# Layer 0 of a four-layer network: impulse answers as small products, a woven expert front, norm sums at the writer, fills after attention

## The chip, the cores and the metric

One core of one Trainium2 chip runs the whole network in one launch. The metric is device time in microseconds (us), from the first to the last instruction of the execution. The engines are TensorE (PE: matrix products, PEld: its weight loads), VectorE (DVE), ScalarE (ACT), GpSimd (POOL) and SyncE (SP, which here only issues DMAs). Each engine works through its own instructions strictly in order; semaphores tie the engines together.

## The reference, cut to what matters

The input x has 32 sequences of 256 positions with 128 channels. Four layers each add an attention-like branch and an expert branch. The change touches layer 0 and the first lines of layer 1. In layer 0 the branches are:

- **Attention branch.** with xn the layer norm of x, `h` is a second layer norm of xn (with gamma and beta), and x becomes x + xn + y. y comes from h: a projection to three parts of 256 channels each, `u`, `v`, `g`. `u` goes through a depthwise convolution over 3 positions and a Silu, and then through a long convolution over time with one impulse answer per channel: `k_c(t) = sum over n of B[c,n] C[c,n] exp(-exp(A[c,n]) t)`, 64 states n, with `D[c]` added at t = 0. The result is gated (`y * sigmoid(g) + silu(v)`, the sigmoid made as (1 + tanh(g/2))/2) and projected by `out_w`. The reference writes the convolution as a scan over time: `s = s * eA + u * B; y = sum(s * C) + u * D`.
- **Expert branch.** A layer norm of x gives xn. A gate (`xn @ gate_w`, softmax over 16 experts) scores every token; each expert takes its 32 best tokens of each sequence, applies `Wd(gelu(Wg xn) * Wu xn)` with 256 hidden channels, scales by the score and adds it to those tokens. A shared expert of the same form runs on all tokens.

Layer 1's attention begins with a layer norm of x once more. The expert branches of layers 1 and 3 need tables of rows in DRAM ("slots") that start blank.

## The kernel before, in words

x stays in SBUF for the whole run, as 64 tiles of 128 tokens by 128 channels; a **block** is 4 tiles (2 sequences, 512 tokens), and there are 16 blocks. In `l0_attn` a `manual_schedule` (L497) keeps PE, ACT and DVE in the order in which the program is written; in `l0_ffn` a scheduler orders them before the change, which is why DVE's small constants (same_e, sel_b, rep) stand among the operations of the norm there. Waits come from the tiles: a pool with n buffers lets a name be written again when the reader of n writes ago is done, and a pool that is closed leaves its room to the next pool, whose first writers then wait for the last readers of the old one.

**Slots and fills** (`Slots.fill`, L274 to L282). The two slot tables are blanked by 56 DMAs of 260 KB, all issued by POOL. Each step is an `iota` into one of two blank tiles (L278) and a DMA from it (L282). The pool of the blank tiles is opened ahead of layer 0, and the call stands near the top of `l0_attn`.

**Norms** (`Norm`). `take` runs one `bn_stats` per tile (L214); `close(lo, hi)` turns the sums of the tiles lo to hi into mean and reciprocal root by some 20 small DVE operations (L220 to L248), 38 where the norm is a double one (`double=True`, which also gives r2). `ln_stats` is a take of all 64 tiles and one close. `normed` (L113) applies it to one tile, `transpose4` (L120) turns a block on PE.

**`l0_attn`.** Prelude: the loads; `a_t` through an Exp; `stats(0, 8)`; the products of the convolution's and the projection's weights (`wc`, L608); and small tables split in three bf16 parts. The impulse answers are made by `wave` (L571: an ACT Exp of 128x256 for each state n and half c of the channels) and `gather` (L578: a DVE multiply-add of it into `kk`), 64 of each for each half c, spread over loop 1 (c = 0) and loop 2 (c = 1). Each finished half goes to DRAM (`kpad`, L586), from where `fetch` (L675) reads it back in shifted rows. The loops over the 16 blocks are:

1. `prepare(blk)`: `normed`, x's own update on ACT (L632), transposes, and hT with gamma and beta (L638); then `project(0, blk - 1)`: 24 products with three shifts of hT (L652) and 4 with the bias rows (L655), and Silu into `us[0]` (L659). Between them stand a gather for each block, groups of waves, and the norm sums of the tiles 32 to 63 at block 2.
2. `project(1, blk)`, waves and gathers for c = 1, and `respond(0, blk)` (L685: 32 products with 32 columns of weights, tz fetched).
3. For c = 0 and 1: `gate` (v, g: L745, L746; Silu and Tanh, L749 and L751; z on DVE, L755 and L758), `give` one block later (L764 and L768 on PE, x's add on DVE, L773); for c = 0 also `respond(1, blk)`.

**`l0_ffn`.** A norm of all of x (`ln_stats`), then the gate for all 16 blocks (normed, transposes, xnT copied by ACT at L850, `lg` on PE at L852), one softmax; then four groups of 8 sequences, each `choose` (the 32 best by max, index and replace, L878 to L882, and a table `tab` of positions and scores, L887 to L901) followed by four `shared` blocks (g and u L911 and L912, gelu L913, product L914, o L918, x's add L923). Then for each of the 32 sequences the picking: `ib` (L955) spreads the chosen positions over the partitions, DVE turns it into 0/1 masks (`pick`, L962), and two products with xn gather the rows (`xg`, L965) into `xs` (ACT, L968). Then 16 experts in two halves each (L989 to L996), and the scattering (transposes L1008; `put` masks L1011, one of four on POOL; products L1019; x's add L1024). Layer 1 begins with a double `ln_stats` of x.

Of the kernel before, what the change touches and what calls it, by code (L numbers as in the profile page):

```python
# [19 lines left out]
P = 128  # L20
# [7 lines left out]
class Ctx:  # L28


    def __init__(self, tc, ins, es):
        self.tc, self.nc, self.ins = tc, tc.nc, ins
        nc = self.nc
        self.cp = es.enter_context(tc.tile_pool(name="persist", bufs=1))
        cp = self.cp
        self.x = cp.tile([P, NT, D], F32, name="x_sb")
        self.ident = cp.tile([P, P], F32, name="ident")
        make_identity(nc, self.ident)
        self.ones = cp.tile([1, P], F32, name="ones_row")
        nc.gpsimd.memset(self.ones, 1.0)  # L40

# [449 lines left out]
def l0_attn(K):  # L491
# [3 lines left out]
    with ExitStack() as es:  # L495
# [11 lines left out]
        a_t = K.load(sp, "a0_A", ins["a0_A"].rearrange("(c p) n -> p c n", p=P), [P, 2, NS])  # L507
        b_t = K.load(sp, "a0_B", ins["a0_B"].rearrange("(c p) n -> p c n", p=P), [P, 2, NS])
        c_t = K.load(sp, "a0_C", ins["a0_C"].rearrange("(c p) n -> p c n", p=P), [P, 2, NS])
        cols = K.load(sp, "a0_cols")  # L510
        gamma, beta = cols[:, 0:1], cols[:, 1:2]
        bias_v, bias_g, d_p = cols[:, 2:4], cols[:, 4:6], cols[:, 6:8]
# [8 lines left out]
        for n in range(3):  # L521
# [10 lines left out]
        tt = sp.tile([P, SEQ], F32, name="tt")  # L532
        nc.gpsimd.iota(
            tt, pattern=[[-1, SEQ]], base=SEQ - 1, channel_multiplier=0,
            allow_small_or_imprecise_dtypes=True,
        )
        kk = sp.tile([P, 2, KW], F32, name="kk")
        nc.gpsimd.memset(kk, 0.0)
# [10 lines left out]
        kpad = [dram.tile([P, KW], F32, name=f"kpad{c}") for c in range(2)]  # L549
# [6 lines left out]

        nc.vector.tensor_scalar_min(a_t, a_t, 69.0)
        nc.scalar.activation(a_t, a_t, AF.Exp)
        nc.vector.tensor_scalar_mul(a_t, a_t, -1.0)
        nc.vector.tensor_mul(b_t, b_t, c_t)  # L560
        nc.vector.tensor_scalar_mul(b_t, b_t, 0.5)
        for slots in (K.slots1, K.slots3):
            slots.fill(K.fill_pool)
        waves = {}

        def wave(c, m, pool):

            e = waves[c, m] = pool.tile([P, GC, SEQ], F32, name="tz")
            for i in range(GC):
                n = GC * m + i  # L570
                nc.scalar.activation(e[:, i, :], tt, AF.Exp, scale=a_t[:, c, n : n + 1])  # L571

        def gather(c, m):
            acc = kk[:, c, 0:SEQ]
            e = waves.pop((c, m))
            for i in range(GC):
                n = GC * m + i
                nc.vector.scalar_tensor_tensor(  # L578
                    acc, e[:, i, :], b_t[:, c, n : n + 1], acc, ALU.mult, ALU.add
                )  # L580
            if GC * m + GC == NS:
                k0 = kk[:, c, SEQ - 1 : SEQ]
                nc.vector.scalar_tensor_tensor(
                    k0, d_p[:, c : c + 1], 0.5, k0, ALU.mult, ALU.add
                )
                nc.sync.dma_start(kpad[c], kk[:, c, :])  # L586

        for m in range(6):
            wave(0, m, tp)
# [4 lines left out]
        def stats(lo, hi):  # L594
            for j in range(lo, hi, 8):
                norm.take(K.x, j, j + 8)
            norm.close(lo, hi)
            s = slice(lo, hi)
            nc.vector.tensor_scalar_add(r1[:, s], norm.r[:, s], 1.0)
            nc.vector.scalar_tensor_tensor(  # L600
                nb[:, s], norm.mean[:, s], -1.0, norm.r[:, s], ALU.mult, ALU.mult
            )

        stats(0, 8)


# [13 lines left out]
        es1 = ExitStack()  # L620
# [3 lines left out]
        ew = K.pool(es1, "a0ew", 4)  # L624
# [42 lines left out]
        def fetch(c, g):  # L667
            for q in range(2):
# [4 lines left out]
                    kpad[c].tensor, kpad[c].offset + c0 * KW, [[1, P], [KW, GC], [1, SEQ]]  # L673
# [26 lines left out]
        for m in range(2):  # L700
            gather(0, m)
        stats(8, 32)
        for blk in range(NBLK):
            if blk == 2:
                stats(32, NT)
            prepare(blk)
            if blk:
                project(0, blk - 1)
            if blk in (3, 7, 11):
                for m in range(blk + 3, min(blk + 7, NS // GC)):  # L710
                    wave(0, m, ew)
            if blk + 2 < NS // GC:
                gather(0, blk + 2)
# [3 lines left out]
        for blk in range(NBLK):  # L717
            project(1, blk)
            if blk in (0, 3, 6, 9):
                for m in range(blk * 4 // 3, blk * 4 // 3 + 4):  # L720
                    wave(1, m, ew)
            if blk < 12:
                for m in range(blk * 4 // 3, (blk + 1) * 4 // 3):
                    gather(1, m)
# [36 lines left out]
        def give(c, blk, z):  # L761
# [11 lines left out]
            nc.vector.tensor_add(xb, xb, o)  # L773

        last = None
# [14 lines left out]
def l0_ffn(K):  # L790
    nc, ins = K.nc, K.ins
    NE, CAP, F = 16, 32, 256
    ES = NE * CAP
    with ExitStack() as es:
        sp = K.pool(es, "f0", 1)
        xn = sp.tile([P, NT, D], F32, name="xn")


        idx = sp.tile([P, 4, CAP], F32, name="idx")
        tab = sp.tile([P, 4, 2, 8, 4], F32, name="tab")  # L800
# [4 lines left out]
        mean, r = K.ln_stats(sp, K.x, "f0")  # L805
# [7 lines left out]
        sel_b = sp.tile([P, 8, P], F32, name="sel_b")  # L813
# [20 lines left out]
        )  # L834

        with ExitStack() as ts:
            xp = K.pool(ts, "f0x", 1)
            wk = K.pool(ts, "f0w", 2)
            xnT = xp.tile([P, NBLK, 512], F32, name="xnT")
            sc = xp.tile([P, 2, NB, NE], F32, name="sc")  # L840
            with ExitStack() as ps:
                pt = K.pool(ps, "f0pt", 2, PSUM)
                pl = K.pool(ps, "f0pl", 1, PSUM)
                lg = pl.tile([P, 2, NB, NE], F32, name="lg")
                for blk in range(NBLK):
                    for j in range(4 * blk, 4 * blk + 4):
                        K.normed(xn[:, j, :], j, mean, r)
                    t = pt.tile([P, 512], F32, name="t")
                    K.transpose4(t, xn[:, 4 * blk : 4 * blk + 4, :])
                    nc.scalar.copy(xnT[:, blk, :], t)  # L850
                    for i in range(4):
                        nc.tensor.matmul(  # L852
                            lg[:, i % 2, 2 * blk + i // 2, :],
                            xnT[:, blk, i * P : (i + 1) * P], gate_w, start=True, stop=True,
                        )
                K.softmax(
                    xp, sc.rearrange("p h b e -> p (h b) e"), lg.rearrange("p h b e -> p (h b) e")
                )

            pt = K.pool(ts, "f0pt2", 1, PSUM)  # L860
            pg = K.pool(ts, "f0pg", 2, PSUM)
            po = K.pool(ts, "f0po", 2, PSUM)

            def choose(q):

                t = pt.tile([P, SEQ], F32, name="st")
                for h in range(2):
                    nc.tensor.transpose(
                        t[:, h * P : (h + 1) * P],
                        sc[:, h, 8 * q : 8 * q + 8, :].rearrange("p b e -> p (b e)"), K.ident,  # L870
                    )
                s = wk.tile([P, SEQ], F32, name="s")
                nc.vector.tensor_copy(s, t)
# [11 lines left out]
                nc.gpsimd.tensor_copy(idx[:, q, :], vi[:, 0, :])  # L885
                vt = pt.tile([64, P], F32, name="vt")
                nc.tensor.transpose(vt, vi.rearrange("p k s -> p (k s)"), K.ident)  # L887
                vs = wk.tile([64, P], F32, name="vs")
                nc.vector.tensor_copy(vs, vt)
                o = pt.tile([P, 2, P], F32, name="st")  # L890
                for k in range(2):
                    nc.tensor.matmul(
                        o[:, k, :], rep[:, k].rearrange("p a s -> p (a s)"), vs,
# [4 lines left out]
                    own, o.rearrange("p k (n a) -> p (k n) a", a=4),  # L898
# [6 lines left out]
            def shared(blk):  # L905
                h = wk.tile([P, 2, 512], F32, name="h")
                for c in range(2):
# [3 lines left out]
                    nc.tensor.matmul(g, wsg[:, cs], xnT[:, blk, :], start=True, stop=True)  # L911
                    nc.tensor.matmul(u, wsu[:, cs], xnT[:, blk, :], start=True, stop=True)  # L912
                    nc.scalar.activation(h[:, c, :], g, AF.Gelu)  # L913
                    nc.vector.tensor_mul(h[:, c, :], h[:, c, :], u)  # L914
                o = po.tile([P, 4, D], F32, name="o")
# [9 lines left out]
            for q in range(4):  # L925
                choose(q)
                for blk in range(4 * q, 4 * q + 4):
                    shared(blk)


        xs = K.pool(es, "f0s", 1).tile([P, 4, NB, 4, CAP], F32, name="xs")
        ew = K.pool(es, "f0e", 3)

        def expert(e):
            return (
                K.load(ew, "f0_wg", ins["f0_wg"][e]),
                K.load(ew, "f0_wu", ins["f0_wu"][e]),
                K.load(ew, "f0_wd", ins["f0_wd"][e].rearrange("(c p) d -> p c d", p=P), [P, 2, D]),
            )

        experts = [expert(0), expert(1)]
        with ExitStack() as ps:
            gw = K.pool(ps, "f0g", 2)
            pi = K.pool(ps, "f0pi", 2, PSUM)
            px = K.pool(ps, "f0px", 2, PSUM)
            for q in range(4):
                bd = gw.tile([P, NE, CAP], F32, name="bd")
                nc.gpsimd.tensor_mul(
# [1050 lines left out]
```

## Time and profile before

| | before |
|---|---|
| median of 3 runs | 3496.14 us (3491.07 to 3504.56) |
| the profiled execution | 3581.18 us |
| its span | 3579.2 us |
| its mean granted TensorE clock | 0.867 |
| PE, DVE, ACT, POOL busy in it | 2793.4, 1958.5, 1333.5, 821.4 us |
| layer 0 in it | 0 to 876 us (attention to 373, experts from there) |
| stages of attention: prelude; loop 1; loop 2; loop 3 c = 0; c = 1 | 0 to 52; to 156; to 245; to 326; to 372 |
| stages of experts: norm; gate; softmax, choice and shared; picks; experts; scatter | 372 to 392; to 437; to 532; to 622; to 796; to 876 |
| norm of layer 1 | 876 to 896 |

The profiled execution is one of many and took 85 us longer than the median; the durations are read from it. A line such as L768 is a line of the kernel; a group is written out<-in by the program's names, with the shape in partitions x elements. "idle before <-" names what ended the idle time of an engine ahead of an instruction. Idle time of an engine that others don't wait for costs nothing.

### The profile page before, as it was taken

The page shows a single profiled execution, that of the slowest core. Times are in us where ns is not written, and L with a number is a line of the kernel's source. Part 1 is how long each engine was busy: PE and PEld are TensorE (multiplying, and loading weights), DVE is VectorE, ACT ScalarE, POOL GpSimd, SP SyncE. Part 2 cuts the span into 40 slices and gives each one's busy share as a digit, 9 for nine tenths or more (in the row PEclk, how much of TensorE's full clock was granted, in tenths as well). Part 3 has the DMA queues.
Part 4 walks back from the last instruction along what each step waited for, and adds up shares of the span by engine and source line. Part 5 has one row for each costly group of instructions (what it writes and reads, how often), then busy time and mean ns, then how long its engine had stood idle before and what let it go on. Part 6 is the DMA issues. An engine that isn't in the chain of part 4 may idle for free.

```text
span 3579.2 us, 57560 instructions
## 1 busy us (share of the span) xinstructions
PE 2793.4 (78%) x21538; PEld 1924.2 (54%) x21538; DVE 1958.5 (55%) x4453; ACT 1333.5 (37%) x2765; POOL 821.4 (23%) x1025
## 2 busy tenths in 40 slices
PE   2999799997978339996399999967888988962660
PEld 2765563447556228996266666656455555551550
DVE  7535564347673003444756666555677777672238
ACT  2753222221623013442055555611256666720120
POOL 4100000004223741553300000002230000046354
PEclk9999599999988668998599999958889999955795
DMA  6487000100010100224344444200144444301132
GB/s 173 137 255 224 27 1 0 36 23 4 1 54 17 47 32 27 72 72 126 86 122 129 128 127 122 74 3 5 48 130 134 121 121 136 82 27 43 51 90 78
DMA packets 248948, 285.00 MB, mean 80 GB/s; under 512 B 28387, under 2 KB 224480, under 8 KB 240480
## 3 DMA queue, kind: packets, MB, share of 16 engines
q1 hardware_dynamic: 210080, 228.45, 22.2%
q0 software_dynamic: 17792, 42.40, 3.7%
q10 hardware_dynamic: 20800, 10.49, 1.2%
q8 instruction: 171, 2.80, 0.3%
q14 instruction: 105, 0.86, 0.1%
HBM read 156.69 MB, written 122.45 MB: 78 GB/s over the span
## 4 chain that ended last, share of the span: by engine, by line
PE 40%; DVE 12%; another core or an unknown queue 6%; issue 6%; POOL 5%; ACT 4%; DMA 2%; POOLq 0%; ACTq 0%; SPq 0%; DVEq 0%
PE t L1456 7%; PE o L1476 6%; POOL f_back L377 4%; PE s L1401 3%; PE m L1488 2%; DVE top L1414 2%; PE m L1361 2%; PE hp L425 2%; DVE y L113 2%; PE o L441 2%; ACT e L1464 2%; PE m L1388 1%; PE t L120 1%; PE t L1337 1%
## 5 line engine op out<-in xcount | busy, mean ns | idle before, releaser
L1414 DVE TENSOR_REDUCE top<-s 128x6 f32<-128x768 f32 (+1 forms) x512 | 556.2, 1089 | 252.3 <-PE t L1337 90.9
L1464 ACT ACTIVATE e<-t 128x384 f32<-128x384 f32 (+1 forms) x1024 | 508.6, 546 | 173.3 <-PE t L1337 102.0
L1456 PE MATMUL t<-q,k 64*128 64x256 f32 (+1 forms) x2048 | 418.2, 305 | 38.3 <-ACT e L1464 37.4
L1401 PE MATMUL s<-k,q 48*128 48x256 f32 (+1 forms) x2048 | 419.3, 328 | 4.0 <-DVE top L1414 3.7
L1456 PEld LDWEIGHTS t<-q,k 64*128 64x128 f32 x2048 | 291.9, 188 | 155.5 <-ACT e L1464 91.9
L1476 PE MATMUL o<-e,val 128*32 128x256 f32 (+1 forms) x4096 | 301.5, 367 | 0.1
L1401 PEld LDWEIGHTS s<-k,q 48*128 48x128 f32 x2048 | 292.2, 195 | 11.2 <-DVE top L1414 8.0
L377 POOL DMA_INDIRECT f_back<-y,place x224 | 218.7, 976 | 221.3 <-DVE y L446 174.1
L431 ACT ACTIVATE h<-hp,w 128x256 f32<-128x256 f32 x368 | 154.3, 470 | 245.3 <-PE hp L425 193.0
L425 PE MATMUL hp<-xT,w 128*128 128x256 f32 x736 | 185.9, 392 | 32.1 <-DVE xT L416 20.9
L441 PE MATMUL o<-w,h 128*128 128x128 f32 x1472 | 184.1, 277 | 0.0
L120 PE MATMUL t<-ident,xn 128*128 128x128 f32 x320 | 73.9, 364 | 137.0 <-DVE xn L113 117.3
L441 PEld LDWEIGHTS o<-w,h 128*128 128x128 f32 x1472 | 175.0, 193 | 0.1
L425 PEld LDWEIGHTS hp<-xT,w 128*128 128x128 f32 x736 | 134.2, 195 | 53.1 <-DVE xT L416 24.8
L1596 POOL TENSOR_SCALAR xn<-x_sb,mean_a,r_a 128x128 f32<-128x128 f32 x64 | 56.0, 883 | 461.8 <-PE m L1350 444.3
L1215 PE MATMUL o<-w_all,h 128*128 128x128 f32 x512 | 71.3, 293 | 115.6 <-ACT h L1211 106.7
L1337 PE MATMUL s<-hideq,pick 64*128 64x128 bf16 x1024 | 145.3, 229 | 0.0
L1337 PE MATMUL t<-hidek,pick 64*128 64x128 bf16 x1024 | 144.7, 224 | 0.0
L120 PEld LDWEIGHTS t<-ident,xn 128*128 128x128 f32 x320 | 54.7, 194 | 164.7 <-issue 123.3
L1215 PEld LDWEIGHTS o<-w_all,h 128*128 128x128 f32 x512 | 68.1, 207 | 135.4 <-ACT h L1211 114.5
L371 POOL DMA_INDIRECT f_rows<-row,slot x128 | 122.8, 960 | 40.4 <-issue 36.6
L652 PE MATMUL up<-wc,hT 128*128 128x128 f32 x768 | 127.3, 306 | 0.0
(475 smaller groups left out, 5606.5 us busy)
## 6 DMA issues: line engine op xcount, KB each, us to landing
d<-half SPq DMA_DIRECT2D x256, 256.0 KB
tz<-kpad SPq DMA_DIRECT2D x64, 512.0 KB
q<-d SPq DMA_DIRECT2D x128, 256.0 KB
k<-d SPq DMA_DIRECT2D x128, 256.0 KB
f_rows<-blank POOLq DMA_DIRECT2D x56, 260.0 KB
xs<-f_rows SPq DMA_DIRECT2D x112, 130.0 KB
y_d<-ys SPq DMA_DIRECT2D x32, 256.0 KB
yt<-y_d SPq DMA_DIRECT2D x32, 256.0 KB
```

The costliest lines, as they stand in the source:

```text
L120: self.nc.tensor.transpose(ps[:, i * P : (i + 1) * P], xn[:, i, :], self.ident)
L377: i = self.K.nc.gpsimd.indirect_dma_start(self.back, bass.IndirectOffsetOnAxis(ap=place, axis=0), row, None)
L425: nc.tensor.matmul(hp[:, i, :], w[:, (c + i) * P : (c + i + 1) * P], xT, start=True, stop=True,)
L431: nc.scalar.activation(h[:, c + i, :], hp[:, i, :], act, bias=w[:, b1 : b1 + 1])
L441: nc.tensor.matmul(o[:, i, :], h[:, c, i * P : (i + 1) * P], w[:, F + c * D : F + c * D + D], start=c == 0, stop=c == FC - 1,)
L1215: nc.tensor.matmul(o[:, i, :], h[:, c, i * P : (i + 1) * P], w[:, F + c * D : F + c * D + D], start=c == 0, stop=c == FC - 1,)
L1337: nc.tensor.matmul(t.rearrange("p (n q) -> p n q", n=3)[:, 0:3:2, 64 * n : 64 * n + 64], pick[r, n, :], hide[name][r], start=False, stop=n ...
L1401: nc.tensor.matmul(s[:, j, lo:hi], q[r, p, h * P : (h + 1) * P], k[r, p, 0 : hi - lo], start=h == 0, stop=not causal and h == 1,)
L1414: nc.vector.tensor_reduce(tops[b][:, :, :, p].rearrange("q h j -> q j h"), out_of["s"][:, :, 0:used].rearrange("q j (h k) -> q j h k", h=n ...
L1456: nc.tensor.matmul(t[:, kh * SEQ : kh * SEQ + SEQ - late], k[r, p, kh * P : (kh + 1) * P], q[r, p, late:SEQ], start=kh == 0, stop=not caus ...
L1464: nc.scalar.activation(e, t, AF.Exp)
L1476: nc.tensor.matmul(o[32 * i : 32 * i + 32, late:SEQ], val[b % RING][:, kh, 4 * g + i, :], exps[4 * g + i][:, kh * SEQ : kh * SEQ + SEQ - l ...
```

## The change

What it does, part by part:

- **Impulse answers.** `wave` and `gather` go. With t = 16 a + b the exponential splits in two factors: `waves[0]` (b, in single steps) and `waves[1]` (a, in steps of 16), each 128x2048, in the room of `us[1]`, with A, B and C packed by the host so that two sets of 64 states lie on the partitions. `twice` is waves[1] times B C / 2. A channel's answer is then one product with 64 rows, 32 columns of weights and 16 columns of the other factor; `impulse(h)` makes 128 channels so, and sends them to `kpad` by four DMAs. It stands at blocks 1 and 2 of loop 1, ahead of `project`.
- **Norms.** Loop 1 takes the sums in groups of 4 tiles and closes 16 at a time (`finish`, at blocks 3, 7 and 11, after `prepare`). The norm of the experts is taken in `give` for c = 1 (`following`, closed every fourth block), and layer 1's norm in the scattering loop (`sums`, closed every eighth sequence). Both `ln_stats` go. `K.next_norm()` hands out two norms in turn, both double.
- **Experts' front.** Under a hand-written order (`manual_schedule` for PE, ACT and DVE) the gate runs 4 blocks ahead of `shared`; `score` and `choose` work on 4 blocks; the lower product of a shared block comes one block later; picks follow 4 blocks behind, `take` one sequence behind `pick`. xn is made by ACT in place of DVE; `sel_b` and `bd` are bf16. The PSUM pools are pt 2, pl 1, pg 1 (g, u and o), px 2 (for ib and xg together).
- **Experts and scattering.** The lower product comes one half later. All four `put` are made by DVE, the pools have three buffers, and `give` comes one sequence later, the norm sums two.
- **Fills.** They stand after `l0_attn`, in a pool of their own that is opened when l0_attn's pools are closed.

The diff, cut to its core:

```diff
@@ Ctx
+        self.norms = [Norm(self, cp, f"x{i}", True) for i in range(2)]
...
@@ l0_attn
-        for slots in (K.slots1, K.slots3):
-            slots.fill(K.fill_pool)
...
+        E = 16
+        for c in range(2):
+            nc.scalar.dma_start(kpad[c * P : (c + 1) * P, SEQ:], nothing)
+        for i in range(GC):
+            at = 32 * i + E - 1
+            nc.scalar.dma_start(d_m[at : at + 1, :], ins["a0_D"][i : i + 1, :])
...
+        room = us[1].rearrange("p c h b -> p (c h b)")
+        for k, wave in enumerate(waves):
+            nc.vector.tensor_mul(
+                wave, a_t.unsqueeze(2).to_broadcast([P, P, E]),
+                back[:, k : k + 1, :].to_broadcast([P, P, E]),
+            )
+            nc.scalar.activation(wave, wave, AF.Exp)
...
+        def impulse(h):
+            kp = pk.tile([P, P // GC, E], F32, name="kp")
+            rows = slice(64 * h, 64 * h + 64)
+            for q in range(P // GC):
+                for i in range(GC):
+                    c = GC * q + i
+                    nc.tensor.matmul(
+                        kp[32 * i : 32 * i + 32, q, :],
+                        twice[rows, c].rearrange("p k e -> p (k e)"),
+                        waves[0][rows, c, :], start=True, stop=True,
+                        tile_position=(64 * h, 32 * i),
+                    )
...
+            for i in range(GC):
+                dst = bass.AP(
+                    kpad.tensor, kpad.offset + (h * P + i) * KW, [[E, E], [GC * KW, P // GC], [1, E]]
+                )
+                nc.sync.dma_start(dst, kk[32 * i : 32 * i + E])
...
-        for m in range(2):
-            gather(0, m)
-        stats(8, 32)
         for blk in range(NBLK):
-            if blk == 2:
-                stats(32, NT)
             prepare(blk)
+            if blk in (1, 2):
+                impulse(blk - 1)
             if blk:
                 project(0, blk - 1)
-            if blk in (3, 7, 11):
-                for m in range(blk + 3, min(blk + 7, NS // GC)):
-                    wave(0, m, ew)
-            if blk + 2 < NS // GC:
-                gather(0, blk + 2)
+            if blk + 4 < NBLK:
+                norm.take(K.x, 4 * blk + 16, 4 * blk + 20)
+                if blk % 4 == 3:
+                    finish(4 * blk + 4, 4 * blk + 20)
...
@@ give
             nc.vector.tensor_add(xb, xb, o)
+            if c == 1:
+                following.take(K.x, 4 * blk, 4 * blk + 4)
+                if blk % 4 == 3:
+                    following.close(4 * blk - 12, 4 * blk + 4)
...
@@ l0_ffn
+        nmr = sp.tile([P, NT], F32, name="nmr")
+        nc.vector.scalar_tensor_tensor(nmr, norm.mean, -1.0, norm.r, ALU.mult, ALU.mult)
...
+            for blk in range(LEAD):
+                gate(blk)
+            for blk in range(NBLK + 4):
+                q = blk // 4
+                if blk % 4 == 0 and q < 4:
+                    sc = score(q)
+                if blk < NBLK:
+                    if blk + LEAD < NBLK:
+                        gate(blk + LEAD)
+                    h = shared(blk)
+                    if risen:
+                        lower(*risen)
+                    risen = (blk, h)
...
+                if blk % 4 == 1 and q < 4:
+                    vi = choose(q, turn(sc))
+                if blk % 4 == 3 and q < 4:
+                    table(q, vi)
+                for b in range(2 * (blk - 4), 2 * (blk - 4) + 2):
+                    if b >= 0:
+                        p = pick(b)
+                        if picked:
+                            take(*picked)
+                        picked = (b, p)
...
@@ the scattering
-                    (nc.vector if g else nc.gpsimd).tensor_scalar(
+                    nc.vector.tensor_scalar(
...
+            def sums(b):
+                norm.take(K.x, 2 * b, 2 * b + 2)
+                if b % 8 == 7:
+                    norm.close(2 * b - 14, 2 * b + 2)
...
@@ l1_attn
-        mean, _, r2 = K.ln_stats(sp, K.x, "a1", double=True)
+        mean, r2 = K.norm_of_x.mean, K.norm_of_x.r2
...
@@ build
-        fill = es.enter_context(ExitStack())
-        K.fill_pool = K.pool(fill, "fill", 1)
         for f in STAGES if stages is None else stages:
             f(K)
             if f is l0_attn:
-                fill.close()
+                with ExitStack() as fs:
+                    pool = K.pool(fs, "fill", 1)
+                    K.slots1.fill(pool)
+                    K.slots3.fill(pool)
```

## The prediction

> **What bounds the kernel now.** The page first, its busy row in 40 slices (89.5 us each). Layer 0 fills slices 0 to 9, and TensorE (PE) is busy in almost all of them:
>
> ```profile
> PE   2999799997978339996399999967888988962660
> ...
> POOL 4100000004223741553300000002230000046354
> PEclk9999599999988668998599999958889999955795
> ```
>
> The reader is to see two things: POOL (GpSimd) works in slices 0 and 1 only, so the fills that stand there cost PE nothing; and the clock is at half in slice 4. The view of windows, cut at layer 0's stages, says the same in us (columns: window, its length, PE, PE weight load, VectorE (DVE), ScalarE (ACT), POOL, granted clock, DMA share, GB/s):
>
> ```profile
> 156.00:245.00 89.00, 89.00 (x984) 68.30 (x987) 35.72 (x73) 57.80 (x114) 0.00 (x0) 1.00 0.73 225
> 326.00:372.00 46.00, 44.57 (x210) 27.87 (x210) 33.67 (x51) 22.67 (x33) 0.00 (x0) 1.00 0.32 97
> 372.00:392.00 20.00, 0.51 (x5) 0.35 (x4) 19.17 (x95) 0.00 (x0) 0.44 (x2) 0.54 0.27 79
> 392.00:440.00 48.00, 44.31 (x193) 38.81 (x192) 18.12 (x64) 10.82 (x18) 0.00 (x0) 0.50 0.00 1
> 623.00:795.00 172.00, 172.00 (x383) 69.78 (x382) 65.32 (x95) 38.21 (x64) 0.00 (x0) 1.00 0.10 30
> ```
>
> PE sets the end in these stages but in 372 to 392 (norm sums alone on DVE), and 392 to 440 runs at half clock. (From 245 to 326 DMA sets it, B below.) Then the timeline at layer 0's seams (start, us, engine, line; in brackets the idle time before and its releaser):
>
> ```profile
> 12.51 0.17 DVE L234 TENSOR_TENSOR mean_a<-st_a 128x8 f32<-128x8 f32 x1
> ...
> 20.30 0.17 DVE L248 TENSOR_TENSOR r_a<-r_a,r_a 128x8 f32<-128x8 f32 x1
> ...
> 76.18 1.24 PE L120 MATMUL t<-ident,xn 128*128 128x128 f32 x4 [11.65 <-DVE xn L113]
> ...
> 371.21 1.13 PE L768 MATMUL o<-w_a_out_w,z 128*128 128x128 f32 x8 [1.43 <-DVE z L758]
> ...
> 391.83 2.01 PE L120 MATMUL t<-ident,xn 128*128 128x128 f32 x8 [19.49 <-issue]
> ```
>
> A close of a norm takes 12.51 to 20.47, 8 us, though it has only 8 columns; while one runs PE starves (11.65 us at 64.5). The fills and the impulse answers, by tile and by form:
>
> ```profile
> L282 POOL DMA_DIRECT2D f_rows<-blank x56: 767/767/997, 5.7 to 121.0; - x56
> ```
>
> ```profile
> L578 DVE SCALAR_TENSOR_TENSOR kk<-tz,w_a_B,kk 128x256 f32<-128x256 f32 x64 | 30.9, 482 | 9.7 <-ACT tz L571 4.6
> L571 ACT ACTIVATE tz<-tt,w_a_A 128x256 f32<-128x256 f32 x64 | 26.0, 493 | 0.9 <-DVE w_a_A L559 0.9
> ...
> L278 POOL IOTA blank<- 128x4 f32 x56 | 7.5, 134 | 44.7 <-DMA f_rows<-blank 44.3
> ```
>
> POOL waits 44.3 us for the two blank buffers. From 25.21 (first fill of a steady row) to 121.0 are 50 steps: **1.92 us a fill**.
>
> [...] an operation of a close is 0.17 us at 8 columns and about 0.2 apart at 8, 24 and 32. So a close costs 8 us whatever its width, and a norm cut in four pays it four times. [...] after 19.5 us idle the clock stays at .50 from 375 to 443 although PE is 92% busy. [...] the trace has 32 such loads in 1.24 us, 39 ns each, which I use.
>
> **The change part by part.** Stages are against before's times; + is later.
>
> *A, prepare loop (52 to 155.8).* Removed: 64 of 128 gathers (30.9 us DVE) and 64 waves (26.0 us ACT). Of these only four PE stalls come back: 11.65 (second close) and 1.3, 1.1, 1.1 (gather behind waves): 15, plus about 5 of half clock after. Added: (1) In the prelude, wave and twice products of 128x2048 (1.22 us for 1024 elements, so 2.4 each, four) and two Exp of about 2: 14 us; ACT's first Exp also queues behind six small DMAs, four of which wait for x's DMAs. Off go 4 gathers' groups and the close of 24. First transpose stays near 52. (2) 512 passes of 64x32 weights into 16 columns; at 39 ns each 10 us a half, [...] both halves stand ahead of a projection in PE order: +20. The 8 impulse DMAs to kpad on SP are in 64-byte runs, but nothing reads kpad before 156. (3) Three closes, at blocks 3, 7, 11, in DVE order between hT(blk) and xn(blk+1). The gap from transpose to transpose is then hT .81 + take .79 + close 8.1 + xn 1.11 = 10.8 against the 4.1 of one projection: 6.5 idle, three times, 19.5, and 2.3 of half clock each, 7. In all: first transposes 51.5, second 4.3 later, impulse 10 and 2 for a cold clock, a cold projection 6, impulse and projection 16: 90 at the block after,  + 13 x .43 + 14 x 4.1 = 63, + 26.5 = 179 against 155.8: **+24** (5 to 37).
>
> *B.* Second projection and c = 0 of the gates: PE and DMA set them (4.10 + 1.43 = 5.53 a block; DMA share .99 at 300). The other 64 gathers and waves lay beside PE (DVE 35.72 and ACT 57.80 of 89 us), so taking them off is worth **0**.
>
> *C, gates c = 1 (326 to 372).* PE 2.61 a block; DVE has .72 + .72 + .68 = 2.15. The takes add 4 x .198 = .79: 2.9, so DVE becomes the bound, +.3 x 16 = 5. Three of four closes (8 us, double) stand in DVE's queue ahead of later z, on which each give waits: +24. **+28** (20 to 33). The fourth falls under the fill.
>
> *E, seam to l0_ffn.* The fills come after l0_attn and take the room its pools leave. In the built order of the changed kernel the first blank memset (POOL) waits for the last give's product, and the first tiles of l0_ffn lie where blank lay: nmr (DVE), the gate's xn (ACT), gate_w (SP) and so the logits wait for the last fills' DMAs. Behind nmr queue all of DVE, behind xn all of ACT; tok and pos queue on POOL. So nothing runs meanwhile: 1.5 + 55 x 1.92 + .77 + 2.8 to land = 111, + 2 to the first transpose: 113 after the last give where before had 19.5 + 1.1. **+93** (75 at 1.6 a fill, were the DMA engines, empty now, quicker; 97). The 56 steps taken out of 5.7 to 121 bring nothing: the DMA share there was .46 and PE waited for none of them. POOL's earlier constants move up, unused. SP issues the first nine expert weights ahead of gate_w, beside the fill: 0; without that cover nine times the .45 us of an issue, 4.
>
> *F, FFN front (391.8 to 622.65 = 231).* PE work: gates 4 x 2.86 at half clock + 12 x 1.3; shared 16 x 5.16; picks 32 x (.215 + 4 x .43 = 1.94), ib being one bf16 pass in place of two; tables 4: 176. Not all is had: with a one-buffer g, u and o, and ib and xg sharing two, each choice (6.4 us of max, index and replace, in order on DVE) holds the gelu products and picks behind it; I take 3 + 3 x 6 = 21, tables 6, single buffers .5 x 16 + .3 x 32 = 8 + take waiting for its copy; together 39, so 215: **-15** (-55 at the PE sum, +5).
>
> *G, experts.* The lower product one half later takes off .25 of each 5.41: **-7** (-9 to -3).
>
> *H, scatter and next norm (795.8 to 896.1).* DVE now 4 puts .40 + add .42 + 2 takes .40 = 2.43 a sequence, 78, and four closes, 33: 111 against 100.3: **+10** (0 to 15). POOL's 1.27 us puts go, unmissed.
>
> Sum +24 +28 +93 -15 -7 +10 = **+133**, against the profiled execution's 3579.2 span (3581.18 in all): 3714. That execution is 85 us over the median of the runs, at a granted clock of .867; what I add is mostly waiting on DVE and DMA, which carries over unscaled, so 3496 + 133 = **3629**.
>
> **Rivals.**
> 1. *Not slower: the fill is hidden.* Idle POOL (124 to 370) runs it under attention, or FFN does not touch its room. Then E is -20 and the sum +20, 3516; with F at its PE sum, -20, 3476. It decides from a fill begun 93 us or more before the last give. For it: POOL's 250.7 us of idle; a DMA share of .32 at 326 to 372. Against: the memset's wait for the last give, and the shared room. Chance .06.
> 2. *Closes hide.* DVE runs ahead, A loses 20, C 24, H 10: +79, 3575. Against: hT(blk) before and xn(blk+1) after the close in one in-order queue. Chance .15.
> 3. *The weave chokes.* Single PSUM buffers, F at +20, and a close costs 10: +175, 3671. Chance .17.
> 4. *The impulse is not what the words say*: [...] hidden under DVE's prelude, A near +5: 3610. Chance .12; inside the main range.
>
> **How the numbers follow.** Main case .50, with the rivals' .06, .15, .17, .12. About 0.5% (17 us) is what a measurement of this kernel can tell from no change. Faster: most of rival 1, .04; same .03; slower .93. All best ends together give +36, all worst +187; neither is likely, and I take 3560 to 3675, which leaves out rival 1 and the outer thirds of rivals 2 and 3.
>
> **What would show it.** L282's fills in one unbroken row of 105 to 110 us starting after the last give, PE, DVE and ACT idle beside it and the gate's first transposes at its end; PE idle some 6.5 us before three transposes of loop 1; the last give 45 to 55 us later than 371; the gate at half clock again; FFN front 200 to 220 from first transposes to the first expert product. Wrong if fills overlap attention, if the row is under 90 us, if loop 1 ends before 165, or if the front takes 180.

## The result and the profile after

| | before | after |
|---|---|---|
| median | 3500.35 us (4 runs) | 3695.59 us (4 runs, 3692.79 to 3707.81) |
| ratio | | 1.0558, 95% interval 1.0508 to 1.0608 |
| span of the profiled execution, its clock | 3579.2 us, .867 | 3706.1 us, .853 |

The change costs 195 us where 133 were forecast, and the time lies above the range. The two spans differ by 127 us only, because of what comes after layer 0: 2682.6 us in before's profiled execution, 2616.4 in after's, and the change touches nothing there. A gap of that size was measured between chips: on the chip of the last experiment below the kernel before itself had a median of 3594.62, where it had 3495 to 3504 on those of the others, and a changed kernel took 2685.2 us after layer 0. So this section compares stages and not spans. Their sum, +193.1, agrees with the 195 of the medians. By first and last products of PE:

| stage, ends at | before | after | measured | forecast |
|---|---|---|---|---|
| A prelude and loop 1, first answer product of loop 2 | 159.9 | 179.4 | +19.5 | +24 |
| B loop 2 and c = 0, last answer product | 323.9 | 343.4 | 0 | 0 |
| C gates c = 1, last give | 372.1 | 423.4 | +31.8 | +28 |
| E seam, first transposes of the experts' gate | 391.8 | 536.9 | +93.8 | +93 |
| F front, first expert product | 622.6 | 823.8 | **+56.1** | **-15** |
| G experts, first transposes of the scattering | 795.8 | 988.6 | -8.4 | -7 |
| H scattering and norm, first transposes of layer 1 | 896.6 | 1089.7 | +.3 | +10 |

Six stages are within 10 us of the forecast; the front is off by 71.

The page of after, the same three of its rows (40 slices, 92.7 us each):

```profile
PE   3899317789989793699639999987779888876560
...
POOL 0000230000003147355330001000150000015664
PEclk9899658899988797699858999995879999985695
```

POOL's work has moved from slices 0 and 1 to 4 and 5, and there PE has a 3 and a 1. Slices 6 to 8 are the front: PE at 7 to 8 tenths and not 9 as before. Windows of after (window, length, PE, PE weight load, DVE, ACT, POOL, clock, DMA share, GB/s):

```profile
347.00:424.00 77.00, 51.45 (x202) 30.57 (x200) 65.20 (x229) 21.99 (x32) 0.15 (x1) 0.84 0.19 55
424.00:537.00 113.00, 0.06 (x1) 0.06 (x1) 9.19 (x48) 0.60 (x2) 52.76 (x118) 0.51 0.47 143
537.00:814.00 277.00, 218.31 (x745) 116.74 (x746) 108.96 (x225) 80.35 (x150) 0.00 (x0) 0.84 0.01 2
```

In the middle row three engines all but stand still for 113 us while POOL issues (DVE's 9 us are the fourth close, at the row's start). The last row is the miss: PE 218 of 277 us busy, at a clock of .84. The fills by tile, and the timeline of after at the seam (start, us, engine, line; in brackets the idle time and its releaser):

```profile
L290 POOL DMA_DIRECT2D f_rows<-blank x56: 767/767/997, 425.3 to 532.6; - x56
```

```profile
422.52 1.13 PE L790 MATMUL o<-w_a_out_w,z 128*128 128x128 f32 x8 [1.43 <-DVE z L780]
...
423.85 1.01 POOL L282 MEMSET blank<- 128x520 f32 x2 [418.21 <-PE o L790]
...
536.01 0.23 DVE L837 SCALAR_TENSOR_TENSOR nmr<-mean_x,r_x 128x64 f32<-128x64 f32 x1 [102.47 <-DMA f_rows<-blank]
...
536.40 1.65 ACT L893 ACTIVATE xn<-x_sb,nmr,r_x 128x128 f32<-128x128 f32 x4 [115.47 <-DVE nmr L837]
...
536.94 1.64 PE L128 MATMUL t<-ident,xn 128*128 128x128 f32 x4 [113.29 <-ACT xn L893]
```

The memset goes 1.3 us after the last give begins, nmr 3.4 us after the last DMA is issued, and PE follows within a microsecond: the chain of the forecast, link by link. A fill takes 107.3 / 55 = 1.95 us with little else on the DMA engines (1.2 of the 16.1 MB moved in the middle row).

The timeline of after in attention, loop 1 first and then a close in the gates:

```profile
54.13 3.07 PE L606 MATMUL kp<-u 64*32 64x16 f32 x215
58.66 0.76 PE L606 MATMUL kp<-u 64*32 64x16 f32 x41 [1.46 <-issue]
...
89.95 1.15 PE L128 MATMUL t<-ident,xn 128*128 128x128 f32 x4 [6.25 <-DVE xn L121]
```

```profile
364.06 0.19 DVE L242 TENSOR_TENSOR mean_x<-st_x 128x16 f32<-128x16 f32 x1
...
371.79 0.17 DVE L256 TENSOR_TENSOR r_x<-r_x,r_x 128x16 f32<-128x16 f32 x1
371.88 0.68 DVE L777 SCALAR_TENSOR_TENSOR z<-th,yt 128x512 f32<-128x512 f32 x1
...
373.44 1.83 PE L790 MATMUL o<-w_a_out_w,z 128*128 128x128 f32 x7 [7.92 <-DVE z L780]
```

A close of 16 columns holds z up for 7.8 us, and PE's give waits 7.92 for it. In the front, a block with its gaps, and one of the gaps that a choice leaves:

```profile
654.08 1.65 ACT L893 ACTIVATE xn<-x_sb,nmr,r_x 128x128 f32<-128x128 f32 x4
...
654.62 1.48 PE L128 MATMUL t<-ident,xn 128*128 128x128 f32 x4 [1.07 <-ACT xn L893]
...
656.78 1.06 PE L905 MATMUL lg<-w_f_gate_w,xT 128*128 128x16 f32 x8 [0.68 <-ACT xT L900]
...
657.70 1.50 PE L977 MATMUL g<-xT,w_f_wsg 128*128 128x512 f32 x2
658.99 1.91 PE L978 MATMUL u<-xT,w_f_wsu 128*128 128x512 f32 x2
...
708.45 3.78 PE L1012 MATMUL xg<-pick,xn 128*128 128x512 f32 x4 [5.30 <-DVE pick L1003]
```

Four transposes take 1.48 us (.60 at 572.82, where xn is ready), because xn comes one tile at a time from ACT. Behind gaps of 1.07 and .68 us the two passes of u take 1.91 us. After the 5.30 us for the choice four passes take 3.78, where 1.98 is usual; the granted clock was .60 from 657.7 to 660.7 and .50 from 708.4 to 712.3. But the gaps alone do not settle the rate of what follows. The block at 691 has the same two, and its passes take 1.10 and 1.02 us at a granted clock of 1.00:

```profile
691.16 1.48 PE L128 MATMUL t<-ident,xn 128*128 128x128 f32 x4 [1.07 <-ACT xn L893]
...
693.31 1.06 PE L905 MATMUL lg<-w_f_gate_w,xT 128*128 128x16 f32 x8 [0.68 <-ACT xT L900]
694.23 1.10 PE L977 MATMUL g<-xT,w_f_wsg 128*128 128x512 f32 x2
695.17 1.02 PE L978 MATMUL u<-xT,w_f_wsu 128*128 128x512 f32 x2
```

Of the 16 shared blocks of the front, 9 have passes of g or u near half rate (the slowest two of each take 1.91 to 2.06 us) and 7 have none (1.02 to 1.13).

### The profile page after: what moved, and what is told of

It is laid out like the page before. It is cut to its first block, busy times and chain, and to the rows that moved or that the text cites. A ratio compares the mean times of both kernels' runs of the same rounds, so it can differ in the third digit from the quotient of the medians.

```text
span 3706.1 us, 58322 instructions
## 1 busy us (share of the span) xinstructions
PE 2827.4 (76%) x22018; PEld 1950.2 (53%) x22018; DVE 1945.6 (52%) x4611; ACT 1307.3 (35%) x2700; POOL 775.1 (21%) x987
## 4 chain that ended last, share of the span: by engine, by line
PE 59%; DVE 16%; DMA 8%; POOL 6%; issue 5%; ACT 5%; SPq 0%; ACTq 0%; POOLq 0%; DVEq 0%
PE t L1563 7%; PE o L1583 5%; PE hp L433 4%; PE o L449 4%; PE up L684 3%; POOL f_rows L379 3%; PE s L1508 3%; DMA f_rows<-blank 3%; PE m L1595 2%; PE m L1468 2%; DVE top L1521 2%; POOL f_back L385 2%; PE xg L1012 2%; DVE y L121 2%; DMA f_rows<-row,slot 2%
## 5 line engine op out<-in xcount | busy, mean ns | idle before, releaser
L1508 PEld LDWEIGHTS s<-k,q 48*128 48x128 f32 x2048 | 294.0, 197 | 11.4 <-DVE top L1521 8.0
L415 DVE COPY w<-w_all 128x1028 f32 (+1 forms) x112 | 67.9, 606 | 131.2 <-DMA f_rows<-row,slot 90.7
L684 PE MATMUL up<-wc,hT 128*128 128x128 f32 x768 | 134.8, 319 | 0.0
L684 PEld LDWEIGHTS up<-wc,hT 128*128 128x128 f32 x768 | 110.2, 216 | 10.4 <-issue 2.8
## 6 DMA issues: line engine op xcount, KB each, us to landing
d<-half SPq DMA_DIRECT2D x256, 256.0 KB
q<-d SPq DMA_DIRECT2D x128, 256.0 KB
k<-d SPq DMA_DIRECT2D x128, 256.0 KB
y_d<-ys SPq DMA_DIRECT2D x32, 256.0 KB
yt<-y_d SPq DMA_DIRECT2D x32, 256.0 KB
```

Of the source, the lines that this page charges most:

```text
L684: nc.tensor.matmul(o, hT[:, 2 * blk + b, s : s + P], wc[:, j, cs], start=j == 0, stop=False)
L1508: nc.tensor.matmul(s[:, j, lo:hi], q[r, p, h * P : (h + 1) * P], k[r, p, 0 : hi - lo], start=h == 0, stop=not causal and h == 1,)
```

## The experiments

Each was run beside the kernel before on the same chip; what it gained is its ratio against after's 1.0558, times 3500, and beside it stands the stage in its trace. After's own interval is .005 either way, 17 us, so the times alone show no gain under about 20 us; there the stage has to carry it. How much a stage scatters is seen where it was left alone: with late fills and an unchanged loop 1, A ends between 175.3 and 179.4; with unchanged gates C takes 78.4 to 80.4; and the front of after takes 281.4 to 290.4 us in the five traces that have it, with PE idle for 59.6 to 60.1 us in each and busy for 221.8 to 230.8.

**The front of before, put back in after**: gate, softmax, choice, shared and picks as in the old code; the rest as changed.

```diff
-            for blk in range(NBLK + 4):      # woven front
...
+        mean, r = K.norm_of_x.mean, K.norm_of_x.r
+        ...                                  # the old front
+        es.enter_context(K.tc.manual_schedule(...))   # experts and scattering
```

> The changed kernel with the front of the experts put back as it was before (gate for all 16 blocks, one softmax, choice and shared, then all picks), on the new norm and after the moved fills; experts and scattering as changed. The changed kernel's front took 286.9 us from its first transposes to the first expert product (536.94 to 823.8), before's 230.8. If the weave itself is the cost (its waits between engines and the half clock that they bring), the front is 231 again, give or take 8, and the whole about 56 us under the changed kernel. If the cost came with what stands around it (a clock left cold by the idle of the fill, the room taken over), the old front is slow here too: 255 to 285, and the whole within 30 us of the changed kernel.

Ratio 1.0392 (1.0375 to 1.0410): 58 us less. Its front takes 229.7 us (534.4 to 764.1), though its first products too come after 114.2 us of idle (113.3 in after) and are slow (eight lg in 1.89 us, as in after, where the granted clock was .50 from 536.9 to 557.5; at 656.78 of after eight take 1.06). Its window:

```profile
534.40:764.10 229.70, 221.85 (x797) 130.00 (x797) 120.82 (x271) 50.88 (x83) 5.03 (x8) 0.89 0.01 2
```

The same stage of the kernel before:

```profile
391.80:622.70 230.90, 222.99 (x797) 130.25 (x797) 120.85 (x271) 50.81 (x83) 5.02 (x8) 0.88 0.00 1
```

PE is busy for 221.9 of 229.7 us: the old front has more products and hardly a gap. So the 56 us belong to the new front, its weave with the hand-written order and the PSUM pools that go with it, and not to the slow start or the room.

**ScalarE's order.** xn one block ahead:

```diff
                     h = shared(blk)
+                    if blk + LEAD + 1 < NBLK:
+                        ahead(blk + LEAD + 1)      # the four ACT operations of gate
                     if risen:
                         lower(*risen)
```

> Only ScalarE's order is changed: xn of the gate is made one block earlier, ahead of the lower product and of the copies of the picks. Theory ACT queue: in 12 blocks PE waits 1.07 us for the first xn, and its four transposes are paced by xn (1.48 us in place of .43), 25 us in all, and the half clock that such a gap brings costs again as much on the g and u products behind it: 25 to 45 us less than the changed kernel. Rival PSUM: the single buffers set the pace, the wait only moves to the next product: 0 to 10 us less.

Ratio 1.0485 (1.0468 to 1.0503): 26 us less; front 262.6. PE's idle time on xn in the front (13.8 us in after) is gone, and PE is busy for 212.2 us in place of 226.8. The gain is at the low end: PE's waits for xT grow from 10.8 to 15.5 us, above all in two blocks where a softmax's exponential stands ahead of xT's copy in ACT's queue (2.09 and 2.44 us).

**VectorE's order.** The choice in two halves behind the picks:

```diff
-                for k in range(CAP // 8):
+                for k in range(2 * part, 2 * part + 2):
...
+                if blk % 4 == 1 and q < 4:
+                    made = choose(q, ts_, 0)
+                if blk % 4 == 2 and q < 4:
+                    vi = choose(q, None, 1, made)
```

> The four rounds of a choice are cut in two halves and put on VectorE behind the picks of two blocks, in place of all four ahead of the picks of one. Theory VectorE: PE's four waits for pick masks (2.6 and three times 5.3, 18 us) go, and the half clock behind them, some 2 to 3 us each: 20 to 30 us less. Rival: the choice only comes in the way of the h products of the next block, and PE waits there: within 8 us of the changed kernel.

Ratio 1.0500 (1.0482 to 1.0518): 20 us less; front 256.0. PE's wait for pick masks at the gathers falls from 17.6 to 1.7 us. The ratio's interval overlaps after's, but the front lies well outside its scatter.

**PSUM dealt otherwise.**

```diff
-            pt = K.pool(ts, "f0pt", 2, PSUM)
+            pt = K.pool(ts, "f0pt", 1, PSUM)
-            px = K.pool(ts, "f0px", 2, PSUM)
+            px = K.pool(ts, "f0px", 3, PSUM)
```

> [...] three buffers for ib and xg in place of two, one for the transposes in place of two. Theory PSUM: each take waits for the copy of the one before (.46 us in the tail, about 1.2 at the weight load else), 32 times, 20 us and its clock: 20 to 35 us less. Rival ACT queue: the copies come late because ACT is in order behind other work, so a third buffer brings 0 to 8 us, and the one buffer of the transposes may cost as much.

Ratio 1.0557 (1.0531 to 1.0583): no different. The front of its profiled execution is 272.0. PE is idle for 53.1 us of it, some 7 less than in every trace of the unchanged front, which fits the rival's 0 to 8 and is too little for the times to show; the other 8 us of the difference are busy time. Too few buffers for ib and xg are not what makes the front slow.

**All of the front's waits together**: the two orders above, one ring of four buffers for g, u and o, transposes ahead of the picks and logits behind them.

```diff
+            pt = K.pool(ts, "f0pt", 1, PSUM)
+            pg = K.pool(ts, "f0pg", 4, PSUM)     # one name for g, u and o
...
                     risen = (blk, h)
+                    if blk + LEAD < NBLK:
+                        over(blk + LEAD)         # transposes and xT's copy
...                                               # picks
+                if blk + LEAD < NBLK:
+                    logit(blk + LEAD)
```

> The woven front with its waits taken away together: xn one block ahead on ScalarE, the choice in two halves behind the picks, g, u and o in one ring of four PSUM buffers, the transposes ahead of the picks and the logits behind them; the same work. If these waits and the half clock that they bring are the whole of the 111 us that the front takes over its sum of products at full clock (176), the front falls from 287 to 200 to 215, below the unwoven 231, and the whole is 70 to 85 us under the changed kernel. If something else holds it (weights that load slowly, picks that cost more than their products), it stays at 235 or over: at most 50 us less.

Ratio 1.0354 (1.0310 to 1.0398): 71 us less. The front, in windows of after and then of this kernel:

```profile
536.90:823.80 286.90, 226.79 (x764) 119.98 (x765) 113.29 (x231) 82.80 (x154) 0.00 (x0) 0.85 0.01 2
```

```profile
536.70:746.40 209.70, 191.37 (x764) 111.18 (x765) 113.57 (x231) 82.17 (x154) 0.00 (x0) 0.94 0.01 3
```

The same 764 records of PE: idle time falls from 60.1 to 18.3 us, and busy time from 226.8 to 191.4. So of the 77 us some 42 were waits and some 35 were products running slowly, with the clock at .85 and not .94; 2 of the 16 shared blocks are slow, where 9 were. In the traces the weave now beats the old front by 20 us; by the times it is 13, with intervals that overlap.

**The fills put back** at the top of l0_attn, with their old pool.

> Only the fills are put back to their old place near the top of l0_attn, with their old pool; all else as changed. Theory (exposed fill): the row of 56 DMAs runs beside the prelude and loop 1 again, l0_ffn starts after the last give, the fourth close (8 us) and one chain of nmr, xn and transposes, 12 us, where it now takes 114: about 100 us less than the changed kernel, about 3590. Rival: early fills hold up the new DMAs of the impulse answers and of x, and part comes back in attention: 60 to 85 less.

Ratio 1.0318 (1.0279 to 1.0358): 84 us less. In the trace the seam is 106.0 us shorter and layer 0 ends 102 us earlier (987.7 against 1089.7). So the exposed fill is the seam. The fills now take until 136.7, and the first transposes of loop 1 come at 54.7 in place of 49.9, but the last give comes only .5 us later. Whether early fills cost this kernel more than that is not shown: the 84 has an uncertainty of some 20 us.

**The fills' room kept** until l0_ffn ends, the fills still after l0_attn:

```diff
-                with ExitStack() as fs:
-                    pool = K.pool(fs, "fill", 1)
+                fs = ExitStack()
+                pool = K.pool(fs, "fill", 1)
...
+            if f is l0_ffn:
+                fs.close()
```

> The fills stay after l0_attn, but the pool of the blank tiles is closed only after l0_ffn, so that no tile of l0_ffn lies where they lay; all else as changed. Theory (the shared room holds three engines): the gate starts 12 us after the last give instead of 114, beside the fills, but tok and pos still queue behind the 56 DMAs on GpSimd, so that the first pick, due 70 us after the gate's start, waits some 25 to 30 us for tok: 65 to 80 us less than the changed kernel in the whole. Rival (the fills' own wait or the DMA engines hold the start): less than 15 us.

Ratio 1.0275 (1.0255 to 1.0295): 99 us less, more than forecast. Its timeline at the seam, and tok by tile:

```profile
424.54 0.77 POOL L290 DMA_DIRECT2D f_rows<-blank  x1 [0.29 <-POOL blank L286]
...
425.42 1.63 PE L128 MATMUL t<-ident,xn 128*128 128x128 f32 x4 [6.90 <-ACT xn L893]
```

```profile
L858 POOL IOTA tok<- x1: 142/142/142, 419.8 to 419.8; 128x2 f32 x1
```

The gate starts 7 us after the last give, with the fills (420.2 to 530.9) beside it. tok did not wait: POOL's order is not fixed by hand, and here tok stands ahead of the fills. So neither the fills' wait for the last give nor their DMAs hold the front; the shared room does.

**One close in the gates** in place of four:

```diff
-                if blk % 4 == 3:
-                    following.close(4 * blk - 12, 4 * blk + 4)
+                if blk == NBLK - 1:
+                    following.close(0, NT)
```

> In the gates for c = 1 the sums are taken as changed, but closed once for all 64 tiles after the last block, in place of four closes of 16. With the fills behind it the single close is covered. Theory (a close costs its 38 operations and not its width): three closes of 8 us leave VectorE's row ahead of z, the last give comes 22 to 26 us earlier and the whole is as much less. Rival (the bn_stats of the takes set the pace): 0 to 8 us less.

Ratio 1.0496 (1.0453 to 1.0539): 22 us less, with an interval that overlaps after's; the stage is clear, from the last answer to the last give 51.1 us in place of 80.0. Its window:

```profile
343.00:391.00 48.00, 45.95 (x201) 26.07 (x199) 44.71 (x111) 22.03 (x32) 0.15 (x1) 1.00 0.30 88
```

DVE holds the takes (44.7 of 48 us) and PE is as busy as before the change. Of C's 31.8 us the three closes are 28.9; 2.9 are left for the takes.

**One close in loop 1**, at block 2, beside impulse answers:

```diff
-            if blk + 4 < NBLK:
-                norm.take(K.x, 4 * blk + 16, 4 * blk + 20)
-                if blk % 4 == 3:
-                    finish(4 * blk + 4, 4 * blk + 20)
+            if blk == 1:
+                norm.take(K.x, 16, NT)
+            if blk == 2:
+                finish(16, NT)
```

> In loop 1 the sums of the tiles 16 to 63 are taken at block 1 and closed once at block 2, beside the impulse answers and cold projections, in place of three closes of 16 at blocks 3, 7 and 11; all else as changed. Theory (three closes, each with 6.25 us of idle PE and some 2 us of half clock behind it): the first answer of loop 2 starts 15 to 20 us earlier than 179.4 and the whole is as much less. Rival (the one close is as exposed, where it now stands, as the three): within 6 us.

The first answer of loop 2 comes at 155.0 in place of 179.4, 24 us earlier (20 against the lower end of A's scatter), and 5 earlier than in the kernel before. The ratio, 1.0525 (1.0474 to 1.0576), is 12 us less than after's and its interval too wide to confirm that; the stage is read from one execution.

**Putting it together.** First, the fills early, one close in the gates, one in loop 1, and the mended front:

> Fills at their old place, one close in the gates, the front of e8_front, and in loop 1 the sums of tiles 16 to 63 taken at block 1 and closed once at block 2, beside the impulse answers. By the sum of the stages against the kernel before: loop 1 -5, gates and seam -4, front -20 to -30, experts -8, scattering 0: 35 to 45 us under the kernel before, near 3455. If the parts do not add up (half clock returns elsewhere), between 3480 and 3510.

Ratio .9929 (.9905 to .9952), 25 us under the kernel before and not the 35 to 45 forecast. Layer 0 ends at 863.5 (before 896.6). The parts that did not add up lie in attention: A and the last give are 8 and 11 us later than before, where a few us less were forecast. Second, the old attention in front of the same experts (its norm's sums kept in the tile names that the experts' norm uses, to make room):

> The attention of the kernel before (impulse answers by waves and gathers, fills at the top), with the sums of the experts' norm taken in its last loop and closed once, and behind it the front of e8_front and the changed experts and scattering. Against c_best it tells the impulse products' own worth. If they only cost (two times 5.2 us of PE in loop 1, with nothing given back, since the gathers lay beside PE): 6 to 12 us under c_best, 3459 to 3465. If the gathers' room on VectorE was worth something in loop 1 or 2: as c_best or above it.

Ratio .9876 (.9850 to .9902). That is 18 us under the kernel above, with intervals that just miss each other (.9902, .9905), though its profiled layer 0 ends only .9 us sooner, at 862.6; where the 18 us would lie is not shown. With early fills the new loop 1 (impulse products and one close) shows no gain over the old one. That it costs anything is not shown. Third, the fills late with their own room:

> As c_best, but the fills stay after l0_attn and keep their own room until l0_ffn ends, as in e2_fill_room, so that they run beside the experts' front and the prelude has no fills in it. Theory: in c_best the early fills cost the prelude and loop 1 some 12 us (first transposes at 55.7 in place of 49.9, first answer of loop 2 at 167.7 in place of 155.0 in e9_one_finish), and beside the front they cost nothing: 8 to 14 us under c_best, a ratio to the kernel before of about .986 to .989. Rival: that gap is the free clock's and not the fills': within 4 us of c_best, .991 to .994.

Ratio .9896 (.9871 to .9921), 37 us under the kernel before on that chip. First transposes at 49.9, first answer of loop 2 at 156.5, and the fills lie under the front without a cost to be seen in it (209.7 us, as long as the mended front without fills beside it):

```profile
L290 POOL DMA_DIRECT2D f_rows<-blank x56: 770/770/997, 374.5 to 487.1; - x56
```

Layer 0 ends at 857.0, the earliest of all. By the times it is 12 us under the first of these three, in line with its theory, and 7 over the second, with intervals that overlap both: which of the last two is best isn't settled, and with late fills the impulse products are no loss that can be seen. All three lie below both kernels; below the kernel before by .7 to 1.2%.

## Why the prediction was wrong

- **The step that failed is F**, the sentence "together 39, so 215". 287 was measured. The products' sum of 176 was about right (the mended front has PE busy for 191 us at a clock of .94), but what stands beside it was mis-sized threefold: 111 us and not 39. Of these, 60 were idle time and 51 busy time above the sum, most of it products that ran slowly (35 by the comparison with the mended front). I had the picks behind the choice (17.6 measured where 21 were forecast) and the takes' copies, but not ACT's order: xn of the gate queued behind the copies of the picks, worth 26 us when taken away. And the start of the front, five gates in a chain of ACT and PE and the first softmax, took 20.6 us to the first shared product where I put 11.4 + 1.3.
- **The half clock was charged once and was there in 9 of the 16 shared blocks.** I priced it for the first four gates. The shared block at 616 ran at about half rate (two passes in 2.05 and 1.92 us against 1.02, at a granted clock of .50) though no gap in the 12 us before was longer than 1.67. Nor did every gap bring it: one of 2.62 us ahead of the products at 580.55 did not (1.13 us, at 1.00). What sets it off in the one case and not in the other stays open. By the comparison of the two fronts it is 35 of the 77 us that the mended one saved.
- **Rival 3 had the direction** (the weave chokes) but a third of the size (+20 for F where 56 were measured) and the wrong place: I named single PSUM buffers. A third buffer for ib and xg took some 7 us of idle time away in the trace and gave nothing that the times show; other orders of ACT and DVE gave 26 and 20. The ring for g, u and o was tried only together with the rest, so its own share stays open.
- **E was right to a microsecond** and its cause is shown: give l0_ffn other room, and the wait is gone (99 us less). C was right in size, with parts of 28.9 for the closes and 2.9 for the takes where 24 and 5 were put. Rival 2 falls for A and C; for H it had the sum right.
- **A was right in sum, in part by luck**, since two errors cancel. The stalls are 6.25 us (6.5 forecast). An impulse half takes 5.2 us and not 10: its 256 passes run at 15 ns apart (3.83 us in all), under the 39 ns of the answers' loads that I used. Part of that came back: from the fourth transposes (79.15, forecast 90) to the end of loop 1 it took 96 us and not 89.5.
- **H was over-priced by 10**: the four puts of a sequence take 1.37 us and not 1.60, and the last close runs beside layer 1's first transposes, which it was not expected to. No run tests how the 10 us divide between the two.
- **Small slips that moved nothing.** The worst ends add up to 184 and not 187, and VectorE's three operations in C to 2.12 and not 2.15. A close of 64 columns takes 9.3 us (886.61 to 895.92 in before, at the start of layer 1), so it is not 8 at every width. POOL also works in slice 9, in the scattering, and the early fills are not quite free: in the changed kernel the first transposes come 5 us later with them.

## What to carry to other kernels

Ask where a moved stage's tiles will lie: a pool that is opened where another just closed makes its first writers wait for the other's last DMA, and here that one wait, for nmr, left DVE, ACT and PE idle for 102.5, 115.5 and 113.3 us. Cut a sum of statistics by what the closing costs (38 small operations here, 8 us for 8 or 16 columns and 9.3 for 64), and put one close where PE has work of its own. The weave of several stages here was worth no more than its worst-placed instructions allowed (a new order of ACT alone gave 26 us, one of DVE 20): list for each engine what stands ahead of the instruction that PE will wait for, and look in the trace at the rate of the products behind the gaps as well as at the gaps.

## What the runs showed of the hardware

Gaps of .7 to 2.8 us were followed by products at about half rate in some blocks of the woven front and not in others, so that 9 of its 16 blocks were slow; between two versions with the same PE work the busy time differed by 35 us (226.8 and 191.4, at granted clocks of .85 and .94). Small products with 64 rows, 32 columns of weights and 16 moving columns, spread over four column groups, ran 15 ns apart (256 in 3.83 us). 56 DMAs of 260 KB through two blank tiles took 1.95 us each in after and 1.92 in before from 25.2 to 121.0, both with little else on the DMA engines (14.9 of 16.1 MB moved and 13.5 of 13.7 are fills); five among the loads of before's prelude took 19.5 us (5.73 to 25.21), while 281 GB/s moved. POOL's waits between them in after are for the blank tiles' earlier DMAs (38.2 us in all); that a third tile would make them faster was not tried.
